# Two conditional attention blocks on one core: where the row maxima are split, new durations for the planner, and earlier residual rows for the last batch

## The chip, the cores and the metric

The kernel runs on one core of one Trainium2 chip. A core has five engines that run their own instruction streams and meet at semaphores: PE (matrix multiply, with its weight loads shown apart as PEld), DVE (vector), ACT (scalar), POOL (GpSimd) and SP, which here issues nearly all DMAs. The metric is the device time of one execution in microseconds (us). Three runs of the kernel before took 1379.7, 1371.59 and 1370.99 us; the median is 1371.59 us.

## The reference, cut to what matters

Two blocks run one after the other on x of shape 8 x 512 x 512 (batch, rows, features). Block L0 is an attention with separate softmaxes of queries and keys, so that its attention matrix is only 64 x 64 for each head. Block L1 is ordinary softmax attention with 16 heads of width 32, and it is where the change lies:

```python
xn = layer_norm(x, norm_w, norm_b)
q = (xn @ q_w + q_b).reshape(B, T, 16, 32);  k, v alike
att = einsum('bnhl,bmhl->bnmh', q, k) + (1 - mask) * -1e6
att = softmax(att, axis=2)                    # over the 512 keys m
y = einsum('bnmh,bmhl->bnhl', att, v).reshape(B, T, 512)
scale, shift = split(silu(emb) @ emb_w + emb_b, 2)
h = layer_norm(y, sb_norm_w, sb_norm_b) * (1 + scale) + shift
return x + silu(h) @ out_w + out_b
```

The softmax subtracts the maximum of every row of scores (one for each query and head) before the exponential. The last line adds the block's input x, the residual, and the output bias.

## The kernel before

**Numbers in two halves.** Products that need nearly full fp32 are made of fp32r halves: a value is rounded to a high half (`h`, an ACT copy) and the rest goes to a low half (`l`, a DVE subtraction). A projection (`project`) is 12 matmuls of 512 columns: high x high, high x low, low x high, each over four blocks of 128 features.

**How block L1 runs.** The work goes by groups G = 0 to 31: batch b = G // 4 and four heads. For a group, `l1_qk` projects keys and queries, writes both halves into a tile `hl` (128 x 2 x 512; two buffers) and stores that in DRAM (`dWk`, `dWq`). `l1_stack` loads it back into two stacked tiles `kst` and `qst` (106 rows x 4 heads x 512), in which the halves of one head lie on rows 0 to 95 and the mask on rows 96 and 97.

`l1_max(G)` makes the row maxima. It multiplies rows 0 to 97 (16 matmuls into PSUM banks), and a DVE reduction of each bank gives one column of `nm`, the negated maximum. The maxima have to come into the scores as eight more rows of `qst` (98 to 105): four heads, each in a high and a low half. Before the change two small DVE instructions make the halves out of `nm` in a tile `mi` of 128 x 16 (a cast, then a subtraction), four TensorE transposes bring `mi` into a bank `mp` of 8 x 512, ACT copies this to `aux` (one buffer, shown as `z`), and one DMA on SP's queue writes `aux` to rows 98 to 105 of `qst`, repeated for the four heads. Rows of zeros and ones in `kst` pick the right row for each head.

`l1_att(G)` then makes the scores with all 106 rows, the maxima included, transposed (keys by queries). ACT takes the exponential of each bank into tiles `A` (ten buffers; two of 16 use `bWq` and `bWk`). `l1_av` multiplies with the values, and the sums of the softmax are made by adding the exponentials of the four key blocks, `A<-A,A`, 12 additions for each group, on POOL or DVE as the planner chooses. The maxima of the next group run beside the scores of this one, four steps ahead.

**The last batch.** No group comes behind it, so the kernel ends in a chain: `l1_last` for the last group, in two halves of 256 queries, then for each half `l1_rden`, `l1_y` with a normalization on DVE (`veb` and `rsb`, the reciprocal standard deviation, on POOL), `l1_hidden_half` and `output`. `output` loads the residual rows of 128 x 512 (`x1`, the output of L0 in DRAM), POOL adds the bias `bo`, the 12 matmuls of the projection follow, DVE adds bank and residual, and a DMA stores the result. In the last batch these rows lie in tiles `v`, which hold the values of L1 until the last `l1_av`.

**What sets the order.** The generators above only record operations. `Order.place` (a planner) then simulates all five engines with a duration for each operation (`_takes`), with buffers and dependences, in 12 rounds, and takes the round that ends earliest by its own numbers. `Order.issue` (lines 486 to 503) emits the instructions in the order of the planned starts. So nearly every row of the profile has line L503, and rows are told apart by tile names. Idle time that the planner expects on PE is filled with dummy matmuls (L499). Each engine runs in the emitted order; a change of a duration in `_takes` (lines 509 to 545) can move any instruction of the program. An operation recorded under `order.on("gpsimd", "vector")` may go to either engine; the additions of `A` are such.

Of the kernel before, what the change touches and what calls it, by code (L numbers as in the profile page):

```python
# [14 lines left out]
F32 = mybir.dt.float32  # L15
F32R = mybir.dt.float32r
AF = mybir.ActivationFunctionType
ALU = mybir.AluOpType
AX = mybir.AxisListType

B, S, D, TE = 8, 512, 512, 1024
P = 128
NC = S // P
# [490 lines left out]
def _takes(engine, method, args, kw):  # L514

    out = args[0]
    n = int(np.prod(out.shape[1:]))
    ins = [a for a in args[1:] if isinstance(a, View) or hasattr(a, "shape")]
    n = max([n] + [int(np.prod(a.shape[1:])) for a in ins]) if engine != "PE" else n
    if engine == "PE":  # L520
        if method == "transpose":
            return 108.0 if n > 32 else 62.0
        return max(62.0, n * (0.455 if args[1].dtype == F32R else 1.668))
    if engine == "ACT":
        t = 178.0 + 0.82 * n
        extra = sum(hasattr(kw.get(k), "shape") for k in ("bias", "scale"))
        return t + 93.0 * extra + (195.0 if "accum_out" in kw else 0.0)
    if engine == "DVE":
        if n < 64:
            return 900.0 if args[0].tile.tag == "mi" else 200.0  # L530
        t = 150.0 + 1.045 * n
        if method == "scalar_tensor_tensor":
            t += 65.0
        if method == "tensor_tensor" and not any(isinstance(a, View) and a.tile.pool.psum for a in ins):
            t += 135.0
            if args[0].tile.tag == "A":
                t += 170.0
        if method == "scalar_tensor_tensor" and not any(isinstance(a, View) and a.tile.pool.psum for a in ins):
            t += 200.0
        return t  # L540
    if engine == "POOL":
        if n < 64:
            return 900.0 if ALU.pow in args else 350.0
        return {"tensor_tensor": 2.75, "tensor_scalar": 1.75}.get(method, 1.03) * n
    raise KeyError(engine)


# [1 line left out]
def kernel(ctx: ExitStack, tc: tile.TileContext, x, cond, mask0, mask1, w0, w1, out):  # L549
    real, order = tc.nc, Order(tc)  # L550
    nc = order
# [6 lines left out]
    sm = order.pool(ctx.enter_context(tc.tile_pool(name="sm", bufs=2)), each=2)  # L558
# [7 lines left out]
    def big(tag, name, dtype=F32, shape=(P, 512)):  # L566
        t = sb.tile(list(shape), dtype, name=name, tag=tag, bufs=BUFS[tag])
        if tag == "stk":
            nc.gpsimd.memset(t[:, :, 0:1].bitcast(F32), 0.0)
        return t  # L570

    def bank(tag, name, parts=P):
        tag = {"S": "mm", "ST": "mm", "a": "mm"}.get(tag, tag)
        return ps.tile([parts, 512], F32, name=name, tag=tag, bufs=BANKS[tag])

    def mm_bank(name):
        return bank("mm", name)

    def chunk(i):
        return slice(i * P, (i + 1) * P)  # L580
# [5 lines left out]
    ident = fixed.tile([P, P], F32, name="ident")  # L586
# [51 lines left out]
    W = {"L0": {}, "L1": {}}  # L638
# [143 lines left out]
    def run(gen):  # L782
        for _ in gen:
            pass
# [39 lines left out]
    def project(pt, left, right, lsl, rsl):  # L824
        n = 3 * ND
        i = 0
        for a, r in ((0, 0), (0, 1), (1, 0)):
            for j in range(ND):
                nc.tensor.matmul(
                    pt, left[a][j][:, lsl], right[r][j][:, rsl], start=(i == 0), stop=(i == n - 1)  # L830
                )
                i += 1
                yield MM
# [31 lines left out]
            hl.append(o)  # L865
        st[l, "h", b] = [(hh, hl)]

    def output(l, b, res, dst, chunks=range(NC), per=NC, tag="y"):
        h = st[l, "h", b]
        for c in chunks:  # L870
            xr = big(tag, f"xr{l}{b}{c}")
            nc.sync.dma_start(xr, res[chunk(c), :])
            nc.gpsimd.tensor_tensor(xr, xr, W[l]["bo"], ALU.add)
            op = mm_bank(f"op{l}{b}{c}")
            yield from project(op, h[c // per], W[l]["Wo"], chunk(c % per), full)
            nc.vector.tensor_tensor(xr, xr, op, ALU.add)
            nc.sync.dma_start(dst[chunk(c), :], xr)


    x1 = [dr.tile([S, D], F32, name=f"x1_{b}") for b in range(B)]  # L880
# [158 lines left out]
    def l1_max(G):  # L1039
        q, k = qst[G % 3], kst[G % 3]  # L1040
        nm = sm.tile([P, NC, 4], F32, name=f"nm{G}", tag="nm4")
        for c in range(NC):
            for j in range(4):
                if c or j:
                    yield
                sp = bank("S", f"s{G}{c}{j}")
                nc.tensor.matmul(sp, q[0:98, j, chunk(c)], k[0:98, j, :], start=True, stop=True)
                nc.vector.tensor_reduce(nm[:, c, j : j + 1], sp, AX.X, ALU.max, negate=True)
        mi = sm.tile([P, NC, 2, 4], F32R, name=f"mi{G}", tag="mi")
        nc.vector.tensor_copy(mi[:, :, 0, :], nm)  # L1050
        nc.vector.tensor_tensor(mi[:, :, 1, :], nm, mi[:, :, 0, :].bitcast(F32), ALU.subtract)
        mp = bank("S", f"mp{G}", 8)
        for c in range(NC):
            nc.tensor.transpose(mp[:, chunk(c)], mi[:, c].bitcast(F32).rearrange("p t j -> p (t j)"), ident)
        aux = big("z", f"aux{G}", shape=(8, 512))
        nc.scalar.copy(aux.bitcast(F32R), mp)
        nc.sync.dma_start(
            q[98:106].bitcast(F32), aux.unsqueeze(1).broadcast_to([8, 4, 512])
        )
        st["max"] = G  # L1060
        yield

# [224 lines left out]
    for b in range(B + 1):  # L1287
# [5 lines left out]
        if b == 0:  # L1293
            run(first)
            split_w("L0", "Wv")
            split_w("L0", "Wq")
            prep_cond()
            with order.after(*st["L0", "xs", 1]):
                load_emb("L0", nc.sync)
            l1_cols = load_cols("L1", list(COLS), nc.sync)  # L1300
            run(second)
            run(l0_kn(b))
            split_w("L0", "Wo")
            load_bo("L0")
        else:
            run(mix(l0_y(b - 1), first, 4, 6))
            if last:
                l1_init(0)
                l1_stack(0)
            run(islice(second, 26 if not last else 24))  # L1310
            run(mix(hidden("L0", b - 1, "S"), second, 4, 7))
            tail = output("L0", b - 1, x[b - 1], x1[b - 1])
            if not last:
                run(mix(l0_kn(b), tail, 4, 12))
            else:
                load_x("L1", 1, x1[1])
                tail = mix(values("L1", 0), tail, 13, 12)
                run(mix(l1_max(0), tail, 1, 6))
# [71 lines left out]
    for b in range(B):  # L1390
# [30 lines left out]
        for g in range(4):  # L1421
            G = 4 * b + g
# [16 lines left out]
    b = B - 1  # L1439
    rest = plan[0][0]  # L1440
    halves = (range(0, 2), range(2, 4))
    for u, half in enumerate(halves):
        run(l1_rden(b, "ST", half))
        run(l1_y(b, "ST", half, True))
        run(l1_hidden_half(b, u))
    run(rest)
    for half in halves:
        run(output("L1", b, x1[b], out[b], half, 2, "v"))
    order.place()
    order.issue(real, ident)  # L1450

# [38 lines left out]
```

## Time and profile before

| | before |
|---|---|
| median of three runs | 1371.59 us |
| the profiled execution's own time | 1380.49 us |
| its span | 1378.7 us |
| busy: PE, PEld, DVE | 1353.1, 953.4, 1040.8 us |
| busy: ACT, POOL | 744.8, 685.1 us |
| granted TensorE clock, mean | 0.996 |
| block L0, roughly | up to 520 us |
| block L1, one batch in the steady part | 108.6 us |

All durations of the prediction come from the one profiled execution, whose time is 8.9 us above the median of the three runs. In rows of groups, the numbers after the count are busy time and mean ns of one instruction, then the idle time of the engine before them and what ended it. In rows of waits, the numbers are the sum in us, how often, and the longest. In rows of the timeline, the first two are start and length in us.

### The profile page before, as it was taken

The numbers are of one execution on the slowest core, as the hardware profiler recorded it, in microseconds if no ns is written. First come the engines' busy times: TensorE is split into PE (matmuls) and PEld (weight loads), VectorE is DVE, ScalarE is ACT, GpSimd is POOL, SyncE is SP. The second block draws the span as 40 slices with busy tenths as digits, with TensorE's granted clock in tenths as the row PEclk, the third lists the DMA queues.
The fourth block names the chain that finished last, engine by engine and source line by source line (L and its number), as shares of the span: only waits on it lengthen the run. The fifth ranks groups of instructions, "written<-read, shape, count | busy, mean of one in ns | idle before, by whom it ended". The sixth has DMA issues, their size and how long they took to land.

```text
span 1378.7 us, 21085 instructions
## 1 busy us (share of the span) xinstructions
PE 1353.1 (98%) x7471; PEld 953.4 (69%) x7471; DVE 1040.8 (75%) x1774; ACT 744.8 (54%) x1398; POOL 685.1 (50%) x759
## 2 busy tenths in 40 slices
PE   9999999999999999999999999999999999998998
PEld 7788788888888886566666566566566566564655
DVE  8667576766667778987788787778778868868876
ACT  4333334433345436547747746746745755863674
POOL 7132323225134435766556555657548538634763
PEclk9999999999999999999999999999999999999999
DMA  8321202202132365444363363364363462553222
GB/s 276 139 85 69 92 27 92 70 31 100 61 100 92 126 208 146 124 120 147 98 162 114 90 179 102 88 186 115 107 186 77 145 179 71 150 144 98 77 55 74
DMA packets 77313, 158.80 MB, mean 115 GB/s; under 512 B 8517, under 2 KB 8641, under 8 KB 77185
## 3 DMA queue, kind: packets, MB, share of 16 engines
q1 hardware_dynamic: 77184, 157.46, 38.7%
q8 instruction: 59, 0.97, 0.3%
q14 instruction: 46, 0.37, 0.1%
q10 hardware_dynamic: 24, 0.01, 0.0%
HBM read 104.90 MB, written 50.43 MB: 113 GB/s over the span
## 4 chain that ended last, share of the span: by engine, by line
PE 91%; DMA 3%; DVE 3%; ACT 2%; issue 1%; POOL 0%; SPq 0%; ACTq 0%; POOLq 0%
PE mm L503 91%; DMA qst<-z 1%; ACT mm L503 1%; DVE mi L503 1%; DVE nm L503 1%; DMA qst<-dWq 1%; ACT y L503 1%; DMA rawL0Wk<-in_L_cond_Wk 0%; ACT A L503 0%; DMA dWq<-hl 0%; DVE A L503 0%; DMA rawL0Wv<-in_L_cond_Wv 0%; ACT z L503 0%; ACT xT L503 0%; DVE xc L503 0%
## 5 line engine op out<-in xcount | busy, mean ns | idle before, releaser
L503 POOL TENSOR_TENSOR A<-A,A 128x512 f32<-128x512 f32 x249 | 332.4, 1356 | 218.7 <-PE mm L503 152.8
L503 DVE TENSOR_REDUCE nm<-mm 128x1 f32<-128x512 f32 x512 | 332.7, 683 | 72.7 <-PE mm L503 69.6
L503 ACT ACTIVATE A<-mm 128x512 f32<-128x512 f32 x450 | 251.0, 602 | 144.2 <-PE mm L503 141.1
L503 PE MATMUL mm<-kst,qst 98*128 98x512 f32 x512 | 202.6, 422 | 3.0 <-DMA qst<-dWq 2.5
L503 PE MATMUL mm<-qst,kst 106*128 106x512 f32 (+1 forms) x528 | 192.8, 405 | 2.2 <-DMA qst<-z 2.0
L503 PEld LDWEIGHTS mm<-kst,qst 98*128 98x128 f32 x512 | 96.7, 192 | 73.0 <-issue 19.9
L503 PE MATMUL mm<-A,v 128*32 128x512 f32 (+1 forms) x932 | 144.3, 589 | 0.0
L503 PEld LDWEIGHTS mm<-qst,kst 106*128 106x128 f32 x528 | 97.4, 190 | 53.7 <-issue 15.5
L503 POOL TENSOR_TENSOR y<-y,bo 128x512 f32<-128x512 f32 x60 | 78.0, 1305 | 96.6 <-DMA y<-in_x 94.6
L503 PE MATMUL mm<-Wvh,xT 128*128 128x512 f32 x384 | 119.4, 401 | 0.0
L503 PE MATMUL mm<-xT,Wkh 128*128 128x512 f32 x384 | 115.7, 409 | 1.6 <-DVE xT L503 0.8
L503 ACT ACTIVATE mm<-mm,cols 128x512 f32<-128x512 f32 x62 | 46.6, 752 | 113.6 <-PE mm L503 113.5
L503 POOL TENSOR_SCALAR v<-bWv,cols 128x512 f32<-128x512 f32 x64 | 46.9, 743 | 119.0 <-PE mm L503 118.5
L503 ACT ACTIVATE y<-mm,shL,scL 128x128 f32<-128x128 f32 (+1 forms) x144 | 76.3, 530 | 50.8 <-PE mm L503 48.3
L503 DVE TENSOR_TENSOR A<-A,A 128x512 f32<-128x512 f32 x73 | 84.8, 1172 | 14.9 <-PE mm L503 12.3
L503 PE MATMUL mm<-ident,xc 128*128 128x128 f32 x512 | 89.6, 278 | 4.2 <-ACT mm L503 2.0
L503 PEld LDWEIGHTS mm<-ident,xc 128*128 128x128 f32 x512 | 63.8, 141 | 32.3 <-ACT y L503 6.5
L503 PEld LDWEIGHTS mm<-xT,Wkh 128*128 128x128 f32 x384 | 68.7, 189 | 22.6 <-ACT xT L503 5.4
L503 PEld LDWEIGHTS mm<-Wvh,xT 128*128 128x128 f32 x384 | 71.6, 189 | 16.3 <-issue 1.7
L503 ACT ACTIVATE mm<-mm,shL,scL 128x128 f32<-128x128 f32 (+2 forms) x152 | 76.1, 500 | 7.2 <-PE mm L503 7.2
L503 PE MATMUL mm<-xT,Wqh 128*128 128x512 f32 x256 | 76.5, 399 | 0.3 <-DVE nm L503 0.2
L503 ACT ACTIVATE hl<-mm,cols 128x512 fp32r<-128x512 f32 x64 | 44.0, 687 | 51.3 <-PE mm L503 44.0
(206 smaller groups left out, 2703.8 us busy)
## 6 DMA issues: line engine op xcount, KB each, us to landing
kst<-dWk SPq DMA_DIRECT2D x96, 256.0 KB
qst<-dWq SPq DMA_DIRECT2D x96, 256.0 KB
dWk<-hl SPq DMA_DIRECT2D x32, 512.0 KB
dWq<-hl SPq DMA_DIRECT2D x32, 512.0 KB
xc<-in_x SPq DMA_DIRECT2D x32, 256.0 KB
y<-in_x SPq DMA_DIRECT2D x32, 256.0 KB
x<-y SPq DMA_DIRECT2D x32, 256.0 KB
xc<-x SPq DMA_DIRECT2D x32, 256.0 KB
```

Of the source, the lines that this page charges most:

```text
L503: getattr(engine, method)(*args, **kw)
```

## The change

Four things change.

- The split of the maxima moves behind the transposes. `nm` itself is transposed (4 x 512 in the bank), ACT copies the bank to rows 0 to 3 of `aux` (the high half), and one DVE subtraction of 4 x 512, bank minus these rows, gives the low half in rows 32 to 35. The two DVE instructions on `mi` are gone. Two DMAs, of four rows each, take the place of one of eight.
- Durations in the planner: a DVE addition of two SBUF tiles into `A` costs 180 ns more; on POOL, the power of n columns is 350 + 180 n in place of 900 ns, other small operations 200 in place of 350, a memset 250 in place of 1.03 ns a column, a tensor_tensor 2.65 in place of 2.75 and a tensor_scalar 1.53 in place of 1.75 ns a column.
- For the last batch, the residual rows and their sums with `bo` are recorded in a function of their own (`residuals`) and lie in two tiles `hl`, two chunks each, which are free once the last keys and queries have been stored.
- `output` takes these rows when it is given them, and tiles `y` otherwise.

```diff
@@ _takes
             if args[0].tile.tag == "A":
-                t += 170.0
+                t += 350.0
...
     if engine == "POOL":
         if n < 64:
-            return 900.0 if ALU.pow in args else 350.0
-        return {"tensor_tensor": 2.75, "tensor_scalar": 1.75}.get(method, 1.03) * n
+            return 350.0 + 180.0 * n if ALU.pow in args else 200.0
+        if method == "memset":
+            return 250.0
+        return {"tensor_tensor": 2.65, "tensor_scalar": 1.53}.get(method, 1.03) * n
@@ output
+    def residuals(l, b, res, chunks):
+
+        t = big("hl", f"xr{l}{b}{chunks[0]}", F32R, (P, 2, 512)).bitcast(F32)
+        for i, c in enumerate(chunks):
+            nc.sync.dma_start(t[:, i, :], res[chunk(c), :])
+            nc.gpsimd.tensor_tensor(t[:, i, :], t[:, i, :], W[l]["bo"], ALU.add)
+        return [t[:, i, :] for i in range(2)]
+
-    def output(l, b, res, dst, chunks=range(NC), per=NC, tag="y"):
+    def output(l, b, res, dst, chunks=range(NC), per=NC, ready=None):
         h = st[l, "h", b]
         for c in chunks:
-            xr = big(tag, f"xr{l}{b}{c}")
-            nc.sync.dma_start(xr, res[chunk(c), :])
-            nc.gpsimd.tensor_tensor(xr, xr, W[l]["bo"], ALU.add)
+            if ready:
+                xr = ready[c]
+            else:
+                xr = big("y", f"xr{l}{b}{c}")
+                nc.sync.dma_start(xr, res[chunk(c), :])
+                nc.gpsimd.tensor_tensor(xr, xr, W[l]["bo"], ALU.add)
@@ l1_max
-        mi = sm.tile([P, NC, 2, 4], F32R, name=f"mi{G}", tag="mi")
-        nc.vector.tensor_copy(mi[:, :, 0, :], nm)
-        nc.vector.tensor_tensor(mi[:, :, 1, :], nm, mi[:, :, 0, :].bitcast(F32), ALU.subtract)
-        mp = bank("S", f"mp{G}", 8)
+        mp = bank("S", f"mp{G}", 4)
         for c in range(NC):
-            nc.tensor.transpose(mp[:, chunk(c)], mi[:, c].bitcast(F32).rearrange("p t j -> p (t j)"), ident)
-        aux = big("z", f"aux{G}", shape=(8, 512))
-        nc.scalar.copy(aux.bitcast(F32R), mp)
-        nc.sync.dma_start(
-            q[98:106].bitcast(F32), aux.unsqueeze(1).broadcast_to([8, 4, 512])
-        )
+            nc.tensor.transpose(mp[:, chunk(c)], nm[:, c, :], ident)
+        aux = big("z", f"aux{G}", shape=(36, 512))
+        nc.scalar.copy(aux[0:4].bitcast(F32R), mp)
+        nc.vector.tensor_tensor(aux[32:36].bitcast(F32R), mp, aux[0:4], ALU.subtract)
+        for t in range(2):
+            nc.sync.dma_start(
+                q[98 + 4 * t : 102 + 4 * t].bitcast(F32),
+                aux[32 * t : 32 * t + 4].unsqueeze(1).broadcast_to([4, 4, 512]),
+            )
@@ the last batch
     run(rest)
+    ready = [t for half in halves for t in residuals("L1", b, x1[b], half)]
     for half in halves:
-        run(output("L1", b, x1[b], out[b], half, 2, "v"))
+        run(output("L1", b, x1[b], out[b], half, 2, ready))
```

## The prediction

> **What bounds the kernel now.** I read the busy totals first, then the waits of PE alone, then the tile `mi`, then two stretches of the timeline. The totals of the page, and the waits of PE over the whole span:
>
> ```profile
> PE 1353.1 (98%) x7471; PEld 953.4 (69%) x7471; DVE 1040.8 (75%) x1774; ACT 744.8 (54%) x1398; POOL 685.1 (50%) x759
> ```
> ```profile
> PE mm L503 <- DVE mi L503: 7.2, 2, 6.6
> PE mm L503 <- DMA qst<-dWq: 2.5, 1, 2.5
> PE mm L503 <- ACT mm L503: 2.0, 7, 0.3
> PE mm L503 <- DMA qst<-z: 2.0, 5, 0.8
> ```
>
> PE is the bound. Its idle time is 1378.7 - 1353.1 = 25.6 us. Of it, 3.0 us lie in the first 50 us (PE busy 46.97 there) and about 3.7 us behind the last matmuls. The largest wait is one of 6.6 us for a tiny DVE instruction. The view of tile `mi` (ns, least/median/most) shows what they take, and the timeline shows the long one:
>
> ```profile
> L503 DVE CAST mi<-nm x32: 174/552/8412, 520.5 to 1325.6; 128x16 fp32r<-128x16 f32 x32
> L503 DVE TENSOR_TENSOR mi<-nm,mi x32: 169/1204/1229, 520.8 to 1326.7; 128x16 fp32r<-128x16 f32 x32
> ```
> ```profile
> 1252.57 8.41 DVE L503 CAST mi<-nm 128x16 fp32r<-128x16 f32 x1
> ...
> 1256.02 4.93 POOL L503 TENSOR_TENSOR A<-A,A 128x512 f32<-128x512 f32 x4
> ...
> 1261.01 0.62 DVE L503 TENSOR_TENSOR mi<-nm,mi 128x16 fp32r<-128x16 f32 x1
> ```
>
> With POOL idle both take 0.17 us. Beside POOL's additions the subtraction takes 1.2 us, about one addition (mean 1356 ns). Once the cast stood for 8.41 us, until a train of POOL instructions was through at 1260.95, and PE ran dry.
>
> **How the profile stands to the median.** The profiled execution took 1380.5 us. Without the 7.2 us on `mi`, and without the 2.5 us on `qst<-dWq`, whose stores had come later behind that stall, it would be 1370.8 us. Two of the three runs took 1371.6 and 1371.0, the third 1379.7. I infer, and can't show, that the two had no such stall. The median 1371.6 is then a time without it, and removing the stall gains nothing against the median. That is why I count it at 0 there, though it is the largest number of the profile.
>
> **The change, part by part.**
>
> *Maxima, DVE.* Each of 32 groups loses a cast (mean 848 ns, 27.1 us in all) and a subtraction (1020 ns, 32.6 us), together 59.7 us. It gains a subtraction of 4 x 512 with one input in PSUM. The nearest row is `xT<-mm,xT` (128x512, one input in PSUM, x48): 688 ns, and its spread shows no waiting for POOL. 32 x 0.69 = 22 us. DVE falls by 37.7 us to about 1003. Below, it could be the 405 ns of a small `y<-kc` cast; above, the 1.2 us of an addition that waits for POOL. I take 0.69, the same operands.
>
> [...]
>
> *Maxima, the way to the scores.* Before: cast 0.85, subtraction 1.02, four transposes, ACT copy 0.57, issue 0.72, landing. After: transposes, ACT copy 0.57, subtraction 0.69, second issue 0.72, landing; the first issue lies beside the subtraction (0.72 against 0.69, so 0.03 late). That is 1.87 - 0.69 - 0.03 = 1.15 us shorter. But the subtraction, between copy and DMA, queues on DVE behind a reduction of 0.68, half of which on average is 0.34: 0.8 us shorter. Behind it on DVE wait the next reductions, which free PSUM banks for PE; they lost 1.87 us ahead of them and get 0.69, so nobody there waits longer. The bank `mp` stays taken about 1 us longer, one of eight. PE transposes four columns where it had eight, 128 instructions as before: 0.
>
> PE's waits for these DMAs are 2.0 us in 5 places, so at most 2.0 us are to be won. I take -1.
>
> *Two DMAs.* SP gets 32 issues more of at most 0.72 us, 23 us of a queue that mostly waits. Behind a second issue that waits for DVE stand the loads of the next stacks and the `dWq` stores; they lie microseconds ahead of their use, so 0. No row shows two DMAs of four rows. From below, the second lands with the first. From above, it is a whole transfer more: the chain that ended last has `DMA qst<-z` at 3.50 to 3.75 us, which with the 1.15 us saved makes +2.6 us a group. Nearest is the issue time, 0.72 behind the first, which the sum above has.
>
> [...]
>
> *The last residual rows.* POOL's four `v<-v,bo` (5.5 us) and their four loads go out of the end:
>
> ```profile
> 1350.89 4.22 POOL L503 TENSOR_TENSOR v<-v,bo 128x512 f32<-128x512 f32 x3
> ...
> 1353.91 0.18 DVE L503 BATCH_NORM_AGGREGATE mvb<-stb 128x2 f32<-128x6 f32 x1
> ...
> 1355.20 0.19 POOL L503 TENSOR_SCALAR veb<-mvb 128x2 f32<-128x2 f32 x1
> ...
> 1356.15 1.26 POOL L503 TENSOR_TENSOR v<-v,bo 128x512 f32<-128x512 f32 x1
> ...
> 1356.43 1.72 DVE L503 TENSOR_SCALAR xc<-xc,mvb,rsb 128x512 f32<-128x512 f32 x2
> ```
>
> The variance is ready at 1354.09, and POOL takes it at 1355.20, behind three additions: 1.11 us. Then two DVE instructions take 1.72 where the later pair takes 0.55 and 0.54: 0.63 us beside the fourth addition. PE has only dummy matmuls there (L499, 18 and 12), so up to 1.7 us of it is on the path; what is late next is DVE, busy with the second half from 1354.33 to 1356.5 whatever POOL does. I take -1.5. Above 0, it would cost at most the 5.5 us if POOL met the additions at a worse place; between 1300 and 1340 POOL is busy 27.1 of 40 us, so there is room. The four loads (0.32 us each on SP) wait for `hl`, whose last stores go out at 1295 and 1301. If SP reached them too early, the loads of the last `kst` and `qst` (1302.8 to 1306.9) would stand behind them, up to some 4 us, the `dWq` landing of 4.13 in the chain that ended last. They are not needed before 1367, so I take 0.
>
> *New durations.* They take no time themselves; they move instructions. DVE additions of `A` measure 1172 ns, POOL's 1356: the planner will see POOL cheaper and send it more of the 384 (before 306 and 78). POOL was busy 64.7 us of a batch of 108.6, so it has room. In such a batch PE is busy 107.7 us:
>
> ```profile
> 979.40:1088.00 108.60, 107.68 (x550) 68.28 (x549) 84.92 (x136) 69.11 (x135) 64.69 (x61) 1.00 0.46 129
> ```
>
> So a better order can win at most 0.9 us a batch in idle time, 7 us over eight, and a worse one can lose the like. With DVE a little freer I take -1.
>
> The sum against the profiled execution: 1380.5 - 9.7 - 1 - 1.5 - 1 = 1367.3. Against the median: 1371.6 - 3.5 = 1368.1. I forecast **1368 us**.
>
> **The rivals.**
>
> 1. *No gain* (1371 to 1379). The wait for POOL only changes its place: additions of `A` on DVE already take up to 1.84 us, and the new order may set a DVE instruction of the critical chain behind a train of POOL's. With one stall of 8 us left in the median run: 1379. For it: PE has hardly idle time in a batch, and any new order shuffles it. Against: no small DVE instruction with both operands in SBUF is left on the way of the maxima. The change then doesn't do what it says.
>
> 2. *Slower* (over 1385). The second DMA lands later than the planner believes, which counts its issue at 560 ns and not 717, and the first score matmul of each group waits. Five groups already wait for `qst<-z`, by 0.4 us on average. If every group waited for the 0.72 us of the second issue: 32 x 0.72 = 23 us, 1371.6 + 23 - 1.5 = 1393. It decides for slower from 13.7 / 32 = 0.43 us of PE idle a group. Against: the way before it is 0.8 us shorter.
>
> 3. *A larger gain* (1358 to 1364, or below). All idle time but start, end and the stall counted above is 25.6 - 3.0 - 3.7 - 9.7 = 9.2 us; without it the time is 1362. More than 1% (below 1357.9) needs 4 us out of PE's busy time too, for instance out of banks that DVE frees sooner (weight loads wait 22.3 us for `nm`, mostly hidden).
>
> **How the numbers follow.** About 1% is what a measurement of this kernel can tell from no change (the three runs spread by 0.6%). Chances: forecast (1364 to 1371) 0.45; no gain (1371 to 1379) 0.28; larger gain within 1% (1358 to 1364) 0.10; faster by over 1% 0.07; 1379 to 1385 0.02; slower by over 1% 0.08. That makes 0.07, 0.85 and 0.08. The range 1360 to 1379 leaves out 0.07 and 0.08, the 0.02, and 0.03 of the larger gain: 0.20.
>
> **What would show it.** Right: no `mi` rows; a row `z<-mm,z` near 0.69 us with little spread; DVE near 1003 us; no PE wait over 3 us in L1; waits of PE for `qst<-z` at or below 2 us; `veb` right behind `mvb` at the end; a batch near 108 us. Wrong: waits for `qst<-z` in most groups with some 0.4 us or more (rival 2), a batch over 110 us, or a new DVE instruction that stands for microseconds beside POOL (rival 1).

## The result, and the profile after

The changed kernel takes 1381.1 us (median of 16 runs, 1379.16 to 1384.08), the kernel before 1371.55 us (16 runs, 1370.05 to 1379.7): a ratio of 1.0067 [1.0058, 1.0075]. It is 9.5 us slower. I had forecast 1368 us, 3.5 us faster, with a range up to 1379; the result lies 2 us above that range and on the other side of no change. It stays within the 1% that I had called no measurable change, but sixteen runs of each resolve it.

One inference can be settled at once. Of the 16 runs of before, one took 1379.7 us, all others 1372.6 or less. The median thus has no stall of 8 us on `mi`; but of 115 more runs of before, taken beside the experiments, 18 took 1378 to 1382 us and the others at most 1375.0, which can make the ratios below, each taken against all runs of before in its round, look up to 0.2% better than the medians. Whether all 18 had the stall isn't shown. No kernel with the new split has an execution 7 us or more above its median, while before and three variants that keep `mi` have some; so the split may well remove the stall, which a median can't show. The profiled execution of after took 1379.16 us, its span 1377.4 us; against the profiled one of before (1378.7 us) it looks 1.3 us faster, only because that one has the stall. Whoever compares the two profiles alone reads the wrong sign.

The totals of the page of after:

```profile
PE 1349.6 (98%) x7457; PEld 947.3 (69%) x7457; DVE 1033.4 (75%) x1762; ACT 747.3 (54%) x1398; POOL 670.7 (49%) x739
```

PE is still the bound. DVE lost only 7.4 us, where I had foreseen 37.7. To see where the time is, I cut each profiled span at the start of the first and of the last reduction `nm<-mm` (my working, from the start times in the trace; the first lies at the start of L1, the last in the last group):

| us | up to the first reduction | first to last | from the last to the end |
|---|---|---|---|
| before (with the stall) | 496.5 | 828.5 | 53.8 |
| after | 496.9 | 826.8 | 53.6 |

Block L0 and the end are as they were, to 0.5 us. Without the 9.7 us that I had set down to the stall, the middle of before would be 818.8, and after is 8.0 us longer there. So the loss lies in the steady batches. These are three batches of after (start:end, length, busy us and instructions of PE, PEld, DVE, ACT and POOL, granted clock, DMA share, GB/s; the batch of before in the same view stands in the prediction):

```profile
873.20:983.40 110.20, 107.60 (x550) 67.71 (x549) 86.63 (x136) 69.86 (x135) 61.11 (x57) 1.00 0.47 128
983.40:1093.60 110.20, 107.60 (x549) 67.59 (x548) 86.55 (x136) 69.75 (x134) 60.95 (x57) 1.00 0.45 127
1093.60:1203.90 110.30, 107.71 (x550) 67.76 (x549) 86.75 (x136) 69.93 (x135) 61.13 (x57) 1.00 0.46 128
```

A batch takes 110.2 us where it took 108.6. PE's busy time in it is the same (107.60 against 107.68 us, 550 instructions each), and the clock is full; its idle time has grown, from 0.9 to 2.6 us. Cut at the first reduction of each batch (my working), the six batches between the first and the last are 0.2 to 2.2 us longer than before, together 8.1 us: most of the loss, and the last three by 1.5 to 1.8 each, so it is in the order of the instructions and not an accident.

What PE waits for, over the whole span of after (sum in us, times, longest): the first lines for matmuls, then three lines for weight loads. Above these three stand `issue`, `ACT A` and `DVE nm`, with 118.7, 31.0 and 23.0 us where before had 109.6, 35.7 and 22.3:

```profile
PE mm L503 <- ACT xT L503: 5.4, 11, 0.8
PE mm L503 <- DVE nm L503: 2.4, 4, 0.6
PE mm L503 <- ACT mm L503: 2.2, 8, 0.3
PE mm L503 <- ACT y L503: 2.1, 7, 0.3
```
```profile
PEld mm L503 <- ACT xT L503: 13.8, 22, 1.1
PEld mm L503 <- ACT y L503: 9.4, 20, 0.7
PEld mm L503 <- ACT mm L503: 8.7, 13, 0.8
```

The same three in before:

```profile
PEld mm L503 <- ACT y L503: 6.5, 14, 0.5
PEld mm L503 <- ACT mm L503: 5.8, 11, 0.8
PEld mm L503 <- ACT xT L503: 5.4, 17, 0.7
```

The line `qst<-z`, on which my rival "slower" stood, is gone from the list altogether. Its place at the top is taken by many small waits for ACT. The waits for `y` and `mm` belong to one piece of code, `l1_tail`, which makes the hidden layer of one chunk of 128 rows and which my prediction didn't mention. Four transposes of `xc` go into the four quarters of one PSUM bank (`hp`), and for each quarter ACT then runs two activations, `y<-mm` out of the bank and `mm<-mm` in place. This is that place in the timeline of after (start, length, idle before and what ended it):

```profile
1086.19 0.27 PE L503 MATMUL mm<-ident,xc 128*128 128x128 f32 x1
...
1086.50 0.46 ACT L503 ACTIVATE y<-mm,shL,scL 128x128 f32<-128x128 f32 x1 [2.07 <-PE mm L503]
1087.01 0.14 PEld L503 LDWEIGHTS mm<-ident,xc 128*128 128x128 f32 x1 [0.29 <-ACT y L503]
...
1087.38 0.43 ACT L503 ACTIVATE mm<-mm,shL,scL 128x128 f32<-128x128 f32 x1 [0.42 <-PE mm L503]
1087.86 0.14 PEld L503 LDWEIGHTS mm<-ident,xc 128*128 128x128 f32 x1 [0.60 <-ACT mm L503]
...
1088.23 0.46 ACT L503 ACTIVATE y<-mm,shL,scL 128x128 f32<-128x128 f32 x1 [0.42 <-PE mm L503]
1088.74 0.14 PEld L503 LDWEIGHTS mm<-ident,xc 128*128 128x128 f32 x1 [0.63 <-ACT y L503]
...
1089.11 0.43 ACT L503 ACTIVATE mm<-mm,shL,scL 128x128 f32<-128x128 f32 x1 [0.42 <-PE mm L503]
```

PE and ACT take turns. Each transpose starts 0.05 us after ACT's activation ends, each activation waits 0.42 us for the next transpose, and the transposes come 0.82 to 0.88 us apart, though they write another quarter than the one that ACT is reading. What keeps them apart stands in the program: the brackets go by semaphore events, and each of these weight loads and activations waits for a semaphore that the other engine counts up. The planner counts no dependence here: for a matmul it marks the whole bank as written, for a transpose only its own columns. So it may put activations between the transposes at no cost in its own numbers.

### The profile page after: what moved, and what is told of

The parts are those of the page before. It is cut to its first block, busy times and chain, and to the rows that moved or that the text cites. A ratio compares the mean times of both kernels' runs of the same rounds, so it can differ in the third digit from the quotient of the medians.

```text
span 1377.4 us, 21092 instructions
## 1 busy us (share of the span) xinstructions
PE 1349.6 (98%) x7457; PEld 947.3 (69%) x7457; DVE 1033.4 (75%) x1762; ACT 747.3 (54%) x1398; POOL 670.7 (49%) x739
## 4 chain that ended last, share of the span: by engine, by line
PE 88%; ACT 4%; DVE 3%; issue 2%; POOL 2%; DMA 1%; SPq 0%; POOLq 0%; ACTq 0%; DVEq 0%
PE mm L503 88%; ACT mm L503 2%; DVE nm L503 1%; ACT y L503 1%; DMA qst<-dWq 1%; ACT xc L503 1%; PE mm L499 0%; DVE mm L503 0%; POOL A L503 0%; POOL rsf L503 0%; SPq L503 0%; ACT xT L503 0%; DVE xc L503 0%; DVE z L503 0%; ACT A L503 0%
## 5 line engine op out<-in xcount | busy, mean ns | idle before, releaser
L503 POOL TENSOR_TENSOR A<-A,A 128x512 f32<-128x512 f32 x238 | 324.3, 1385 | 226.5 <-PE mm L503 155.9
L503 DVE TENSOR_REDUCE nm<-mm 128x1 f32<-128x512 f32 x512 | 331.2, 683 | 72.2 <-PE mm L503 68.6
L503 ACT ACTIVATE A<-mm 128x512 f32<-128x512 f32 x450 | 250.0, 600 | 141.7 <-PE mm L503 136.8
L503 PE MATMUL mm<-kst,qst 98*128 98x512 f32 x512 | 200.6, 416 | 2.2 <-DMA qst<-dWq 1.2
L503 PE MATMUL mm<-qst,kst 106*128 106x512 f32 (+1 forms) x528 | 194.0, 409 | 5.5 <-DVE nm L503 2.4
L503 PE MATMUL mm<-A,v 128*32 128x512 f32 (+1 forms) x932 | 141.7, 586 | 0.0
L503 PEld LDWEIGHTS mm<-kst,qst 98*128 98x128 f32 x512 | 96.7, 192 | 59.6 <-issue 25.5
L503 PEld LDWEIGHTS mm<-qst,kst 106*128 106x128 f32 x528 | 96.5, 189 | 56.0 <-issue 13.6
L503 POOL TENSOR_TENSOR y<-y,bo 128x512 f32<-128x512 f32 x60 | 78.2, 1308 | 103.1 <-DMA y<-in_x 86.8
L503 PE MATMUL mm<-xT,Wkh 128*128 128x512 f32 x384 | 115.8, 410 | 6.0 <-ACT xT L503 5.4
L503 PE MATMUL mm<-Wvh,xT 128*128 128x512 f32 x384 | 120.3, 406 | 0.0
L503 ACT ACTIVATE mm<-mm,cols 128x512 f32<-128x512 f32 x62 | 46.6, 752 | 113.0 <-PE mm L503 113.0
L503 DVE TENSOR_TENSOR A<-A,A 128x512 f32<-128x512 f32 x84 | 98.1, 1173 | 8.8 <-ACT A L503 5.6
L503 ACT ACTIVATE y<-mm,shL,scL 128x128 f32<-128x128 f32 (+1 forms) x144 | 76.2, 529 | 50.3 <-PE mm L503 47.7
L503 PE MATMUL mm<-ident,xc 128*128 128x128 f32 x512 | 93.5, 281 | 7.1 <-ACT mm L503 2.2
L503 POOL TENSOR_SCALAR v<-bWv,cols 128x512 f32<-128x512 f32 x64 | 46.2, 731 | 102.2 <-PE mm L503 99.2
L503 PEld LDWEIGHTS mm<-ident,xc 128*128 128x128 f32 x512 | 64.9, 142 | 39.8 <-ACT y L503 9.4
L503 PEld LDWEIGHTS mm<-xT,Wkh 128*128 128x128 f32 x384 | 68.8, 189 | 27.7 <-ACT xT L503 13.8
L503 PEld LDWEIGHTS mm<-Wvh,xT 128*128 128x128 f32 x384 | 71.5, 189 | 16.8 <-issue 1.7
L503 ACT ACTIVATE mm<-mm,shL,scL 128x128 f32<-128x128 f32 (+2 forms) x152 | 76.0, 500 | 10.9 <-PE mm L503 10.9
L503 PE MATMUL mm<-xT,Wqh 128*128 128x512 f32 x256 | 75.4, 400 | 0.2 <-DVE xT L503 0.2
L503 PE MATMUL mm<-Woh,h 128*128 128x512 f32 x224 | 74.1, 418 | 0.5 <-ACT h L503 0.5
```

What stands on the lines that cost most here:

```text
L503: getattr(engine, method)(*args, **kw)
```

## The experiments

The two theories after the result were these. The **order** theory: nothing that the change adds is slow, but it changes the planner's input and so every instruction's place, and the new order loses the time. The **operations** theory: the subtraction or the second DMA loses it itself. The first eight runs divide the change and draw new orders; the rest follow the wait just shown. Each expectation keeps the names that its theories had at the time: A is the order theory, B and C are forms of the operations theory, D is a reason for the loss of run 1, E is the alternation just shown, F any other reason. L510 and L562 are the L503 of the longer files of the experiments.

In runs 1, 2 and 7, the planner places the operations of before, and the kernel is issued in that order.

**1. The split in the old order.** All old instructions keep their places; the operations on `mi` are left out, the subtraction stands right behind ACT's copy and the second DMA behind it.

```diff
+    plan = record(..., split=False);  plan.place()
+    order = record(..., split=True);  order.follow(plan)   # planned starts and buffers of before
+    subtraction: start = end of ACT's copy + 36 ns;  second DMA: start = subtraction + 700 ns
```

> The operations of the new split, run in the order that was planned for the kernel before: every old instruction keeps its place, the two small ones on mi are left out, the subtraction on the transposed rows stands behind the ACT copy and the second DMA behind it. Durations and the end of the last batch are as before. Theory A (the change loses because the planner made another order, and its operations are no dearer): 1366 to 1372 us, no train of POOL additions holds a small DVE instruction, waits of PE for qst<-z at most 2 us. Theory B (the second DMA and the subtraction make the scores wait in every group): 1378 to 1385 us, with waits of PE for qst<-z of some 0.3 us in most of 32 groups.

1385.91 us, 1.0098 [1.0082, 1.0114], above both ranges. In the old order the split is slower still. Here the operations show up in the waits of PE, and in what DVE waits for ahead of the subtraction (tile `z`):

```profile
PE mm L562 <- DMA qst<-z: 8.1, 11, 1.1
PE mm L562 <- DVE z L562: 3.4, 9, 0.6
```
```profile
  ACT z L562: 25.0, 21
```

DVE stands still for 25.0 us in 21 groups, waiting for ACT's copy with the reductions queued behind it. So an order made for `mi` is a bad one for the split, and the operations theory isn't dead here. But it doesn't explain after, whose order was made anew: there DVE waits 1.8 us for that copy (3 times), and PE never for the DMA.

**2. The split and the early residual rows in the old order.** As 1, with the four loads behind the last loads of the stacks and POOL's additions in its gaps.

```diff
+    order = record(..., split=True, early=True);  order.follow(plan)
+    residual loads: behind the last qst load;  additions: next gaps of POOL
```

> The same, and the residual rows of the last batch early in the tiles hl: their four loads stand behind the last stack loads, their four additions in the first gaps that the old plan leaves POOL. Theory A: 1 to 2 us below the run with the split alone, 1364 to 1371 us; veb follows mvb at once at the end. Theory B: no gain over the split alone, since POOL's work at the end was covered, 1378 to 1385 us.

1384.64 us, 1.0090 [1.0072, 1.0107]. That is 1.3 us less than run 1, the size I had given to the end, but the intervals overlap, and the time lies in theory B's range.

**3. Nothing but another draw of the order.** The kernel before, with one nanosecond more for an addition of `A` in the planner. Not one operation differs.

```diff
-                t += 170.0
+                t += 171.0
```

> The kernel before with one duration of the planner changed by 1 ns (additions of A on DVE 171 in place of 170): no operation differs, only the order that comes out of the planner. Theory A: the time moves by several us, either way, at least 2 us off 1371.5. Theory B: 1370 to 1373 us.

1384.57 us, 1.0089 [1.0072, 1.0105]. One nanosecond in the planner costs 13 us on the chip, more than the whole change. Its waits of PE:

```profile
PE mm L503 <- ACT mm L503: 3.9, 12, 0.4
PE mm L503 <- DVE nm L503: 3.1, 7, 1.1
...
PE mm L503 <- ACT y L503: 1.3, 4, 0.3
```

The same two waits for ACT are among them. But waits aren't all of it. The granted clock of its four runs is 0.993 to 0.996, that of the seven runs of before beside them 0.997 to 1.0; in the profiled execution it stands at half in three stretches, of 3.4, 6.8 and 3.4 us. This is the longest (columns as for the batches, the clock third from the end):

```profile
1316.30:1323.10 6.80, 6.67 (x16) 5.25 (x17) 4.88 (x8) 1.37 (x3) 0.81 (x3) 0.50 0.14 39
```

At half the clock PE's matmuls start 0.43 us apart in the profiled execution of before (1316.1 to 1319.5 us), at the full one 0.23 us (1150 to 1180; medians, my working). Half the clock for 13.6 us is then worth up to 6.8 us, my estimate, so that about half of the 13 us may be the clock. What lowers it isn't shown. The profiled execution of after has no such stretch, so its own loss isn't that. What this run does show is that a loss of the size of after's needs no new operation; that after's is of this kind, the later runs have to show.

**4 to 6. Each part alone**, planned anew.

```diff
# durations_alone: the two hunks in _takes, nothing else
# split_alone: the hunk in l1_max, nothing else
# residuals_alone: residuals(), output() and ready, nothing else
```

> The kernel before with all new durations and nothing else; its operations are those of before. Theory A: the time moves by several us, as in the run with 1 ns; a loss of 3 to 10 us is as likely as none. Theory B: 1370 to 1373 us, or a little faster, because the durations are nearer to the measured ones.

> The kernel before with the new split alone, ordered anew by the planner with the old durations. Theory A (a new order costs 9 to 14 us, whatever caused it, and the split is about neutral once the order fits it): 1374 to 1386 us. Theory C (the split itself costs about 14 us, as in the old order, by scores that wait for the second DMA): 1384 to 1390 us, with 8 us or more of PE waits for qst<-z and for DVE z.

> The kernel before with the early residual rows alone, ordered anew with the old durations. The first rounds of the planner see almost the same program, so the steady batches may keep their order. Theory A: if the batches keep 108.7 us, 1369 to 1371 us, 1 to 2 us won at the end; if they change to 110 us or more, 1378 to 1385 us. Theory C: 1369 to 1372 us in any case, since the operations of the batches are those of before.

| | us | ratio |
|---|---|---|
| durations alone | 1380.72 | 1.0062 [1.0047, 1.0077] |
| split alone | 1377.43 | 1.0024 [1.0001, 1.0047] |
| residual rows alone | 1368.31 | 0.9972 [0.9944, 1.0000] |

The durations alone, without a new operation, are as slow as the whole change (their steady batches take 110.9 to 111.8 us). The split alone lies in theory A's range, below C's; the residual rows alone lie 0.7 us below both ranges. The three differences from before, +9.2, +5.9 and -3.2 us, sum to 11.8, where the whole change costs 9.5.

**7. The old order, with the way of the maxima put right.** As 1, but the transposes, the copy and the first DMA move forward by 0.4 to 2.8 us, into the time that `mi` had taken.

```diff
+    by = planned start of the first transpose - (last reduction + 750 ns)
+    transposes, ACT copy, first DMA: start -= by
```

> The new split in the order of the kernel before, as in the run t1_split_old_order, but with the transposes, the ACT copy and the first DMA of each group moved forward by 0.4 to 2.8 us (1.4 on average), to where the maxima are ready, since nothing has to wait for mi any more. Theory D (in the old order the loss came because the transposes kept the place that left 1.9 us for mi, while copy, subtraction and second DMA then added 1.4 us): most of the 13.8 us goes, 1371 to 1377 us, with the waits of PE for qst<-z and DVE z below 4 us of 11.5. Theory C (the second DMA itself is slow): 1380 to 1386 us.

1385.19 us, 1.0074 [1.0047, 1.0102]. The wait for `qst<-z` fell from 8.1 to 1.8 us, the median way from the last reduction to the last landing from 9.06 to 7.97 us (my working), and the time didn't follow. So the late DMAs aren't what makes the old order slow with the split, though the time lies in theory C's range. What does is open. DVE's wait for ACT's copy, ahead of the subtraction, grew from 25.0 us to 42.4 us (25 times); it may have taken the place of the other, which no run tests.

**8. Another draw.** As 3, with 180.

```diff
-                t += 170.0
+                t += 180.0
```

> The kernel before with one duration of the planner changed by 10 ns (180 in place of 170); no operation differs, and the planner's own estimate of this order is lower than that of before. Theory A: several us off 1371.5, more likely slower, 1374 to 1385 us. If the planner's estimate decides: 1366 to 1370 us.

1368.62 us, 0.9957 [0.9934, 0.9981]. This draw is 3 us faster than before, in the range that I had given for the case that the planner's own estimate decides. With 170, 171 and 180 the same operations take 1371.6, 1384.6 and 1368.6 us. The waits of the chunk transposes for ACT (matmuls and weight loads together, my sum, in which a wait of both counts twice) are 14.2, 21.2 and 12.9 us in them, and 23.0 in after and 24.0 with the durations alone. That made them the suspect.

**9 and 10. The transposes of a chunk kept together.** The plan is left as it is; in what is issued, the four transposes of each `hp` bank follow the first at once. This moves three small PE instructions in each of 28 banks and nothing else.

```diff
+        first = {}
+        for o in self.ops:
+            method, args, kw = o.calls[0]
+            if method == "transpose" and re.fullmatch(r"hp\d\d", args[0].tile.name):
+                n, at = first.setdefault(args[0].tile.name, [0, o.start])
+                first[args[0].tile.name][0] += 1
+                o.start = at + n
         return best[0]
```

> The changed kernel in its own order, except that in block L1 the four transposes of one chunk into its bank hp (all four read the same finished tile) stand directly behind the first of them, in place of up to 3.3 us apart with ACT's reads of the same bank between them. Theory E (the loss of the changed kernel is mostly an order in which these transposes and ACT's activations of one bank stand alternately, so that each waits for the other, which the planner doesn't count): the steady batch falls from 110.2 us to about 109, and the time to 1369 to 1375 us. Theory F (the batches are longer for another reason, such as the waits of PE for ACT xT): 1379 to 1382 us.

> The same edit in the kernel before, whose order has fewer such pairs. Theory E: the steady batch falls from 108.7 us by 0.3 to 0.6, the time by 2 to 4 us, 1367 to 1370 us. Theory F: 1371 to 1373 us.

After, with it: 1371.46 us, 0.9998 [0.9985, 1.0011]. Before, with it: 1367.51 us, 0.9977 [0.9956, 0.9999]. This is the central result: the edit gives after 9.6 us, and the loss against before is gone. The same place in the timeline of after with the edit:

```profile
1079.95 0.60 PEld L510 LDWEIGHTS mm<-ident,xc 128*128 128x128 f32 x4
1080.19 0.60 PE L510 MATMUL mm<-ident,xc 128*128 128x128 f32 x4
...
1080.83 0.46 ACT L510 ACTIVATE y<-mm,shL,scL 128x128 f32<-128x128 f32 x1 [2.40 <-PE mm L510]
...
1081.19 0.42 ACT L510 ACTIVATE mm<-mm,shL,scL 128x128 f32<-128x128 f32 x1
```

Four transposes in 0.60 us instead of four over 2.9 us, and ACT's activations follow without a gap. The batch in the same view as above, and the waits of PE:

```profile
983.40:1092.30 108.90, 106.92 (x550) 68.14 (x551) 85.90 (x135) 69.72 (x133) 60.96 (x57) 1.00 0.47 128
```
```profile
PE mm L510 <- ACT xT L510: 5.0, 10, 0.8
PE mm L510 <- DMA out<-y: 3.5, 1, 3.5
```

The batch is back at 108.9 us. Of the 1.3 us that it lost, 0.6 are idle time of PE (2.0 where it was 2.6) and 0.7 are busy time (106.92 where it was 107.60), since four transposes in a row overlap in PE's record (0.60 us for the four, where one alone takes 0.27 to 0.33). Waits of the chunk transposes for ACT are at most 0.1 us where they were 23.0; those for `xT`, which looked larger in the list, stand as they did (5.0 against 5.4) and so weren't the loss.

**11. The same cause, removed in the planner.** After, with the whole bank marked for a transpose as for a matmul.

```diff
-                    if method == "matmul":
+                    if method in ("matmul", "transpose"):
                         box = (*box[:2], 0, 511)
```

> The changed kernel, with the planner told that a transpose writes the whole bank (as it already holds for matmuls), so that it counts such waits itself and makes a new order. Theory E: measured time less the planner's estimate shrinks from 15 us to 5 to 9, and as the estimate is about that of before, 1368 to 1375 us. Theory A (any new order is a draw, mostly to the worse): 1374 to 1386 us.

1373.86 us, 1.0018 [1.0002, 1.0033]; the waits are 0.7 us. This draws a new order, so its 7.2 us are less clean than the 9.6 of run 9, but a second way of removing the alternation gives nearly the same. How far the planner's estimate then was from the measured time, which theory E also named, isn't shown here.

**12. A draw near after.**

```diff
-                t += 350.0
+                t += 345.0
```

> The changed kernel with the duration of an addition of A on DVE 345 in place of 350, nothing else. The planner's estimate falls by 2.8 us. Theory A: the time moves by several us against 1381, either way, 1370 to 1386 us; if the operations of the change set the time, 1379 to 1383 us.

1378.15 us, 1.0044 [1.0030, 1.0058], with batches of 109.2 us: 5 ns in the planner are worth 3 us, and the time lies just below the range for the case that the operations set it.

**13 to 16. The alternation removed under the null and under each part alone.**

```diff
# null171_hp, split_hp, durations_hp, residuals_hp:
# runs 3, 5, 4 and 6 with the edit of run 9
```

> The kernel before with the additions of A on DVE at 171 ns in place of 170 (no operation differs; 1384.6 us without this edit), and the transposes of each chunk of block L1's end stood together. Theory E (alternating transposes and activations are what makes new orders slow): 1371 to 1377 us, batches at or below 109.5 us. Theory A (a new order is slow for many small reasons): 1380 to 1384 us.

> The new split alone, ordered by the planner with the old durations (1377.4 us without this edit), with the transposes of a chunk together. Theory E: at or below 1371 us, since its batch of 109.8 us slips by 2.7 us at the place of those transposes against the plan. If the split itself costs time in every group (the 4 us by which the changed kernel stays above the kernel before when both have this edit): 1371 to 1375 us; if not, 1364 to 1369 us.

> The new durations alone (1380.7 us without this edit), with the transposes of a chunk together. Theory E: 1371 to 1376 us, because its batch of 111 us slips by 2.2 to 3.3 us at that place. If the durations are what keeps the changed kernel 4 us above: at least 1371 us; if they are neutral, 1366 to 1369 us.

> The early residual rows alone, and the transposes of a chunk together: both gains of this study in the order of before. 1362 to 1366 us, 6 to 9 us below the kernel before, if the 3 to 4 us of each add up; 1367 us if they lie on the same path.

| | us without | us with the edit | ratio with it |
|---|---|---|---|
| before | 1371.55 | 1367.51 | 0.9977 [0.9956, 0.9999] |
| null, 171 | 1384.57 | 1375.60 | 1.0006 [0.9982, 1.0029] |
| split alone | 1377.43 | 1366.14 | 0.9940 [0.9918, 0.9962] |
| durations alone | 1380.72 | 1370.02 | 0.9965 [0.9940, 0.9991] |
| residual rows alone | 1368.31 | 1363.78 | 0.9937 [0.9909, 0.9964] |
| after | 1381.10 | 1371.46 | 0.9998 [0.9985, 1.0011] |

The edit gains in every order: 4.0 and 4.5 us in the two that were fastest, 9.0 to 11.3 us in the four slow ones. Theory E's ranges hold but for the durations alone, which lie 1 us below theirs, and for two of the null's batches, which take 110.0 us. The edit doesn't remove the draw: the null is still 8 us slower than before with the same edit. Part of that is the clock. Of the ten runs of the null with the edit, three took 1371.6 to 1372.9 us, at a granted clock of 0.997, and three 1376.2 to 1378.6 us, at 0.992 or 0.993; its mean is 0.995, that of before with the edit 0.998, which I estimate at 4 us. And the sum of the waits isn't the price: the split alone had 14.4 us of them, hardly more than before, and won 11.3. In that order many weight loads wait for a reduction to free a bank instead:

```profile
PEld mm L503 <- DVE nm L503: 44.8, 71, 1.1
```

(before 22.3 us, 38 times.) Those don't come from the alternation one step earlier: with the edit they are 51.7 us, 87 times, in a run that is 11.3 us faster. So a sum of waits doesn't tell what an order costs; the edit does.

**17 and 18. Without the new durations.** After with the edit of run 9, but 170 for 350 (17), and with none of the new durations (18).

```diff
# split_res_poolcost_hp
-                t += 350.0
+                t += 170.0
# split_res_hp: also the old POOL durations
```

> The changed kernel without its longer duration for additions of A on DVE (170 in place of 350; POOL's new durations stay), and with the transposes of a chunk together. It differs from after_hp (1371.5 us) in that one number. If the durations only draw another order: anything from 1360 to 1372 us; the planner's own estimate is its lowest, 7.9 us under that of the changed kernel, so 1360 to 1366 us if the estimate is worth something once the uncounted waits are gone.

> The changed kernel without any of its new durations, and with the transposes of a chunk together: split and early residual rows. If both gains add as in the single runs (1366.1 and 1363.8 us against 1367.5 us for the kernel before with the same edit): 1361 to 1364 us, 8 to 11 us below the kernel before.

1366.06 us, 0.9955 [0.9941, 0.9970], and 1364.48 us, 0.9939 [0.9916, 0.9962]. The one lies just above the range for a planner's estimate that is worth something, the other 0.5 us above the range for two gains that add. The latter, the split and the early rows with the transposes kept together, beats before by 7 us and after by 17 us. The early rows alone do as well (1363.78 us, run 16); the medians can't be told apart, though two of the ten runs of the rows alone, which keep `mi`, took 1372 us, and none of the six with the split more than 1364.9.

## Why the prediction was wrong, point by point

**PE is the bound, and the stall isn't in the median.** Right, as the 16 runs of before show. But what the stall cost wasn't waits alone, as I had it: the granted clock of that execution is at half from 1258.0 to 1264.8 us, a stretch that begins inside PE's wait of 6.6 us, and again for 3.4 us at 1316.

**The order, the step that failed.** I wrote that "a better order can win at most 0.9 us a batch in idle time, 7 us over eight, and a worse one can lose the like", and then took -1. The second half has no ground: a worse order can add any amount of idle time, and after added 1.7 us a batch: 2.6 where there had been 0.9. The durations alone cost +9 us where I had -1. Nor is the first half a bound, because PE's recorded busy time moves with the order: in the order of the residual rows alone the edit takes 4.4 us out of it (1349.5 to 1345.1 us, with the same 7471 matmuls and a full clock in both) and nothing out of the idle time (15.9 and 16.3 us). The evidence for such a loss was in the profile of before: its weight loads waited 6.5 us for `ACT y`, and the chunk transposes 14.2 us in all. I passed over them and didn't ask what the planner thinks of them. Nor did I put a price on the draw itself, which 171 and 180 show to be of the order of 10 us; with it the range would have reached well over 1379 on the slow side.

In numbers, the loss of 9.5 us divides like this. By the edit, the alternation costs after 9.6 us and before 4.0: 5.6 us more. The other 4.0 us are between after and before both with the edit (1371.5 and 1367.5): the split and the early rows take off 3.0 (1364.5), and the new durations then put on 7.0. Of these 7.0, 5.4 come with the one number 350 (1371.5 against 1366.1 in run 17). I take them for the price of the order that they drew. That their values are bad isn't shown: alone, with the edit, the same durations cost 2.5 us (1370.0 against 1367.5), and one nanosecond moved such an order by 8 us (1375.6 against 1367.5, both with the edit), an estimated 4 of them by the clock. Why the order of after stays 4.0 us above is open.

**More additions on POOL.** Wrong in its direction. The additions of two tiles into `A` after, in the groups by line:

```profile
L503 POOL TENSOR_TENSOR A<-A,A 128x512 f32<-128x512 f32 x238 | 324.3, 1385 | 226.5 <-PE mm L503 155.9 <-ACT A L503 68.7 <-DVE A L503 0.7
...
L503 DVE TENSOR_TENSOR A<-A,A 128x512 f32<-128x512 f32 x84 | 98.1, 1173 | 8.8 <-ACT A L503 5.6 <-PE mm L503 2.1
```

With the forms that use `bWk` and `bWq`, POOL has 286 of the 384 and DVE 98, where it was 306 and 78, though DVE's duration had been raised. All additions into `A` without those of `qm` take DVE 98.1 + 15.1 + 6.0 = 119.2 us, where they took 84.8 + 3.1 + 3.7 = 91.6 (by the same groups of before): 27.6 more. The maxima save 59.7 - 21.8 = 37.9 us, as foreseen; 1040.8 - 37.9 + 27.6 = 1030.5, which nearly explains the 1033.4 measured where I had said 1003. What a planner does in sum can't be read from one price.

**The maxima.** The cost of the new operation was right, to 10 ns. The tile `z` of after (ns least, median, most):

```profile
L503 SPq DMA_DIRECT2D qst<-z x64: 637/661/798, 523.1 to 1327.0; - x64
...
L503 DVE TENSOR_TENSOR z<-mm,z x32: 679/680/681, 523.8 to 1326.2; 4x512 fp32r<-4x512 f32 x32
```

All 32 lie within 2 ns of each other, so no wait for POOL, and no cast is left to stall. But the way from the last reduction to the last landing is 8.32 us where it was 8.28 (medians, my working), not 0.8 us shorter. In after the second issue comes 1.33 us behind the first (median), where I had 0.72, since the subtraction queues on DVE behind reductions: it starts 0.55 us behind ACT's copy (median; at most 1.27), where I had allowed 0.34. And the second DMA then takes 3.9 us to land, where the one of eight rows took 3.55. In the order of the split alone the way is 7.10 us, 1.2 shorter, though the second issue comes 1.43 us behind the first there. So the 0.8 was a matter of the order too. The waits of PE for these DMAs did go, from 2.0 to 0 us, as I had said at most.

**The second DMA and the rival "slower".** The forecast's 0 was right in after. Its mechanism, PE waiting for `qst<-z` in most groups, is not there at all. It does appear in run 1, with 8.1 us in 11 places, a third of the 23 us that I had priced. The 3.50 to 3.75 us that I read for `qst<-z` in the chain that ended last leave out two of its five places there, 3.38 and 4.68 us.

**The last residual rows.** Right, and a little larger: from the last reduction to the end it is 51.6 us with the rows alone and 51.3 with rows and edit, against 53.8 and 53.5: 2.1 and 2.2 us, where I took 1.5. The end of after shows the steps:

```profile
1353.55 0.17 DVE L503 BATCH_NORM_AGGREGATE mvb<-stb 128x2 f32<-128x6 f32 x1
...
1353.82 0.19 POOL L503 TENSOR_SCALAR veb<-mvb 128x2 f32<-128x2 f32 x1 [1.51 <-DVE mvb L503]
...
1355.19 1.00 DVE L503 TENSOR_SCALAR xc<-xc,mvb,rsb 128x512 f32<-128x512 f32 x2
```

POOL takes the variance 0.10 us after it is ready (1.11 before), and the pair on DVE takes 1.00 us (1.72). The additions lie at 1315 to 1321. But their loads aren't free, as I took them: two of them stand ahead of the last stack loads, which in after are issued 3.9 us behind the last `dWq` store where it was 1.3 us, and PE waits once for `qst<-dWq`, 1.2 us in after, 0.9 with the rows alone and 1.5 with rows and edit, where before with the edit has no such wait. Yet in after's order the end is 53.6 us, only 0.2 shorter: the two steps are there for DVE and POOL, and the rest of that order gives their gain back. In the two runs with rows, split and edit but without the longer DVE duration (17 and 18) the end even takes 55.6 and 55.4 us. The whole run with the rows alone is 3.2 us faster; what exceeds the end is within the draw.

**The rivals.** "No gain" named a wait that only changes its place, and any new order as its reason; but it looked for the wait at POOL, and it was at ACT, and it put the time at 1379 at most. The sign for a wrong forecast was well chosen: "a batch over 110 us" is what the trace shows.

## What to carry to other kernels

When a planner writes the order, any change of its input is a new draw: before a part is credited or blamed, run a change that touches no operation (one nanosecond here: 13 us) and take its spread into the range. An engine's idle time bounds neither what a new order can lose nor what it can win. Look at the granted clock of both runs before putting a difference down to waits. Look for dependences that the planner doesn't count but the emitted program waits for: the sign is two engines that wait for each other in turn, and mending that gave more than any part of this change.

## What the hardware showed that I hadn't expected

- Transposes into one quarter of a PSUM bank and activations on another quarter ran in turn at the place shown, 0.82 to 0.88 us for each transpose that takes 0.15 us in a row of four. Semaphores of the program hold them apart; what the chip would do without them, no run shows. PE's busy share hides this, since it is 98% in both orders.
- A DMA of four rows landed 3.0 to 3.1 us after its issue, the second of the pair 3.5 to 3.9 us, and the one of eight rows 3.55 (medians, my working). The semaphore of each DMA of four rows counts up at five times (after), that of the one of eight rows at nine (before), the first of them some 1.1 us after the issue and the others from 2.5 us on. The second lands 0.9 us slower than the first in after and 0.4 us slower in the split alone. The delay isn't largest where the second follows soonest: in run 1, where it follows 0.79 us behind the first (1.33 and 1.43 in the other two), it lands only 0.3 us slower (all medians). The cause is open.
- The cast that once stood 8.41 us behind POOL's additions has no successor: in block L1 of after no DVE instruction takes over 2.6 us.
- The granted clock fell to half for 3.4 or 6.8 us at a time, in the profiled execution of null171 for 13.6 us in all, in that of after not at all. Of the ten runs of the null with the edit, those at a mean clock of 0.992 or 0.993 took some 5 us more than those at 0.997.
